# Scaling gathered rows by their decay: twelve ScalarE operations a group against three VectorE operations, from pass 12 on

## The chip, the core and the metric

The kernel runs on one core of a Trainium2 chip. Five engines work side by side, each through its own queue in order: PE (TensorE, matmul and transposition), ACT (ScalarE), DVE (VectorE), POOL (GpSimd, which here issues the gathers) and SP (SyncE, which issues the other transfers). They wait for one another through semaphores. The metric is device time in microseconds (us) of one launch.

## What is computed

One layer of attention over a graph with N = 12,500 nodes, D = 128 features and M = 200,000 edges that are sorted by target node. After a layernorm and a relu (the table `h`), each edge gets a score, decayed by the edge's own weight; per target node the 16 best edges are kept, a softmax is taken over them, and the source rows are summed with these weights:

```python
h = jnp.maximum(_layernorm(x, axis=-1), 0.0)
# in the layer, with node_feats = h:
Qv = node_feats @ W_Q.T
Ku = node_feats @ W_K.T
score = jnp.einsum('md,md->m', Qv[dst], Ku[src]) * (1.0 / np.sqrt(d))
score = score * jnp.exp(-DECAY_LAMBDA * edge_dt)
...
keep = rank < TOPK                      # the 16 best of each target node
w = jnp.where(keep, jnp.exp(score_m - seg_max[dst_s]), 0.0)
alpha = w / jnp.where(denom[dst_s] > 0, denom[dst_s], 1.0)
msgs = node_feats[src_s] @ W_msg.T
agg = jax.ops.segment_sum(alpha[:, None] * msgs, dst_s, num_segments=n)
x = x + jax.nn.relu(node_feats @ W_self.T + agg)
```

The decay multiplies a score, so it may as well multiply the edge's source row of `h` ahead of the product. That multiplication, row by row, is what the change moves.

## The kernel before

Edges are cut into chunks of 128 (one edge per partition) and groups of `GC = 12` chunks: 1,563 chunks, 131 groups. For group g the kernel does this:

- **Gather** (`gather`, line 194, POOL): one indirect DMA per chunk fetches 128 rows of `h_tab` by the edges' indices, which lie in the SBUF table `idx_all`, into `hs`, a tile of 128 x 12 x 128 floats. There are `HB = 10` such tiles. `gather_next(g + 10)` follows the sums of group g, and its first gather waits for the tile to be free.
- **Scale** (`scaled`, line 623, ACT): `hd = hs * dec`, one operation per chunk; the factor is one column of `dec_all`, a number for each partition. `hd` has two tiles.
- **Turn** (`edges_by_turns`, lines 217 and 655): PE transposes four chunks at a time from `hd` into a bank `t` of PSUM, and a copy brings them to `hdT`: the first four chunks by DVE, the others by ACT. Line 659 copies a strip that two groups share.
- **Score and search** (`scores`, `searched`): matmuls into the bank `s`, then DVE finds the 16 best (lines 692 to 703), ACT takes the exponentials (line 707), DVE forms the weights `wt` (713) and the reciprocal of their sum (718, 719).
- **Weights and sums** (`weights_turned`, `weights_out`, `sums`, `means`, `sums_out`): PE transposes `wt`, ACT copies it to `wT` (728), PE multiplies it with the rows in `hs`, ACT scales (753), PE transposes, ACT stores columns to `sum` (768). Blocks of 512 nodes are finished by products and the output on DVE (line 787).

The order on each queue is written out by hand. Passes run from i = -2 to `END = 119`; pass i scores and searches group i, turns group i + 1 and scales group i + 2. The last ten groups have a sequence of their own, in which the first chunks of a group are scaled by ACT and its last four by DVE (line 620). In a pass, `scale(n)` is called with 2, 3, 4, 4 and 12: it takes up to so many of the twelve chunks that are left, so two and three come ahead of the search, and the rest between and after. `T[g]["scaled", j]` keeps the instruction that scaled chunk j: PE's transpositions and the gather that reuses the tile wait for it.

Of the kernel before, what the change touches and what calls it, by code (L numbers as in the profile page):

```python
# [10 lines left out]
F32 = mybir.dt.float32  # L11
# [5 lines left out]
OP = mybir.AluOpType  # L17
# [6 lines left out]
P = 128  # L24
# [9 lines left out]
GC = 12  # L34
# [21 lines left out]
QB = 4  # L56
# [19 lines left out]
def bc(ap, n):  # L76

    return ap.unsqueeze(2).to_broadcast([ap.shape[0], ap.shape[1], n])
# [8 lines left out]
def gnn_layer(  # L87
# [27 lines left out]
    nc = tc.nc  # L115
    N, D = x.shape
# [60 lines left out]
    dec_all = const.tile([P, CW], F32, name="dec_all")  # L177
# [8 lines left out]
    own = [min(GC, CH - GC * g) for g in range(G)]  # L186

    T = [{} for _ in range(G)]
# [16 lines left out]
    def gathers_begun(gs, table, after=None):  # L205

        for g in gs:
            d = gather(g, 0, 1, lambda j: idx_all[:, GC * g + j:GC * g + j + 1], table)
            if after is not None:
                tc.add_manual_dep(d.ins, after.ins.name, SYNC, reason="behind a step of x's norms")  # L210
            gather(g, 1, own[g], lambda j: idx_all[:, GC * g + j:GC * g + j + 1], table)
# [86 lines left out]
    with tc.tile_pool(name="edges", bufs=1) as ep, ExitStack() as stage:  # L298
# [183 lines left out]
        for k in range(DW // FP):  # L482
            c = HALO + FP * k
# [6 lines left out]
        c = HALO + QE  # L490
# [51 lines left out]
    with tc.tile_pool(name="win", bufs=2) as win:  # L542
# [3 lines left out]
        def behind(d, product):  # L546
            if product is not None:
                tc.add_manual_dep(d.ins, product.ins.name, SYNC, reason="behind the last of some products")
# [59 lines left out]
        def load_rels(g):  # L608
            if g % RG == 0:
                d = nc.sync.dma_start(rels[g // RG % 2][0:2 * NQ, :].rearrange("k (g c) -> k g c", g=RG),  # L610
                                  m_rows[g:g + RG, :].rearrange("g (k c) -> k g c", k=2 * NQ))
                if g >= 2 * RG:
                    behind(d, T[g - RG - 1]["scored"])

        def scaled(g, *js, by=None):
            for j in js:
                if j == 0:
                    T[g]["hd"] = win.tile([P, GC, D], F32, name="hd", bufs=2)
                if j < own[g] and by is not None:
                    T[g]["scaled", j] = by(T[g]["hd"][:, j, :], T[g]["hs"][:, j, :],  # L620
                                           dec_all[:, GC * g + j:GC * g + j + 1], None, op0=OP.mult)
                elif j < own[g]:
                    T[g]["scaled", j] = nc.scalar.activation(T[g]["hd"][:, j, :], T[g]["hs"][:, j, :], AF.Copy,  # L623
                                                             scale=dec_all[:, GC * g + j:GC * g + j + 1])
            if g == 1 and 11 in js:
                gathers_begun((RAW + 2,), h_tab, T[1]["scaled", 11])
# [15 lines left out]
        def edges_by_turns(g, c, m=4, by=None, over=False):  # L642

            n = min(m, own[g] - c)
            if n > 0:
                turned_begun(g)
                pt = bank("t", 2)
                for j in range(n):
                    turn(pt[:, j * P:(j + 1) * P], T[g]["hd"][:, c + j, :], ident)
                    if j == 0:  # L650
                        behind(pe["last"], T[g]["scaled", c + n - 1])
                if over:
                    T[g - 1]["over"] = nc.scalar.copy(T[g - 1]["hdT"][:, GC * P:], pt[:, 0:HALO])
                out = by or (nc.vector.tensor_copy if c == 0 else nc.scalar.copy)
                T[g]["turned"] = out(T[g]["hdT"][:, c * P:(c + n) * P], pt[:, 0:n * P])  # L655

        def edges_over(g):
            if g:
                T[g - 1]["over"] = nc.scalar.copy(T[g - 1]["hdT"][:, GC * P:], T[g]["hdT"][:, 0:HALO])  # L659
# [130 lines left out]
        def store(b):  # L790
            o = B[b]["stored"] = B[b]["o"]
            n = min(N, BN * (b + 1)) - BN * b
            full = n // P
            if full:
                nc.sync.dma_start(out[BN * b:BN * b + P * full, :].rearrange("(t p) d -> p t d", p=P), o[:, 0:full, :])
            if n > P * full:
                nc.sync.dma_start(out[BN * b + P * full:BN * b + n, :], o[0:n - P * full, full, :])

        def at(g, stage, *args):
            if 0 <= g < G:  # L800
                stage(g, *args)
# [4 lines left out]
        def blocks(stage, when, i):  # L806
            for b in range(NB):
                if when[b] == i:
                    stage(b)
# [11 lines left out]
        END = G - LATE - 1  # L821
        lags = ((0, (0, 0, 1, 1)),)
        done = {stage: [] for stage in ("scores", "search", "sums", "means", "out")}

        def due(stage, before, i, lag):
            n = len(done[stage])
            while n < len(done[before]) and done[before][n] <= i - lag:
                if stage in ("means", "out"):
                    yield n
                else:  # L830
                    done[stage].append(i)
                    yield n
                n = len(done[stage])

        def some_sums(i, before):
            for g in due("sums", "search", i, before):
                while len(done["means"]) < g - 1:
                    some_means(i, len(done["means"]))
                weights_out(g)
                sums(g)  # L840

        def some_means(i, g):
            while len(done["out"]) < g - 1:
                some_out(i, len(done["out"]))
            means(g)
            done["means"].append(i)

        def some_out(i, g):
            sums_out(g)
            done["out"].append(i)  # L850

        for i in range(-2, END + 1):
            ls, lq, la, lo = [l for k, l in lags if k <= max(i, 0)][-1]
            by_pe = i + 1 >= 0 and True
            if i + 2 >= RG:
                at(i + 2, load_rels)
            blocks(load_h, [None] + need_q[1:], i + 8)
            for b in range(NB):
                if "o" in B[b] and "stored" not in B[b]:
                    store(b)  # L860

            for g in due("out", "means", i, lo):
                some_out(i, g)
            for g in due("means", "sums", i, la):
                some_means(i, g)
            some_sums(i, max(lq, 1))
            blocks(h_out, [None] + need_q[1:], i + 4)
            blocks(q_out, [None] + need_q[1:], i + 2)
            at(i, placed)
            if by_pe:  # L870
                for c in (0, 4, 8):
                    edges_by_turns(i + 1, c)
                edges_over(i + 1)
            unscored = list(range(len(done["scores"]), i + by_pe))

            def some_scores():
                while unscored and unscored[0] - 2 < len(done["search"]):
                    scores(unscored.pop(0), *range(NQ))
                    done["scores"].append(i)

            some_scores()
            turns = list(range(16)) if i + 1 >= 0 and not by_pe else []
            rows = list(range(GC))

            def edges(n):
                if turns:
                    edges_turned(i + 1, *turns[0:n])
                    del turns[0:n]

            def scale(n):  # L890
                if i < END:
                    scaled(i + 2, *rows[0:n])
                    del rows[0:n]

            scale(2)
            if ls == 0:
                edges(4)
                scale(3)
            for g in due("search", "scores", i, ls):
                searched(g, lambda: edges(2))  # L900
                scale(4)
                weights_turned(g)
                some_scores()
            assert not unscored
            edges(6)
            scale(4)
            if lq == 0:
                some_sums(i, 0)
            edges(16)
            scale(GC)  # L910
            if i + 1 > 0 and not by_pe:
                edges_over(i + 1)
            blocks(h_turned, [None] + need_q[1:], i + 6)
            blocks(q_made, [None] + need_q[1:], i + 4)
            for b in range(NB):
                if "po" in B[b] and "o" not in B[b] and B[b]["made"] <= i - lo:
                    output(b)
                if "po" not in B[b] and full_at[b] < len(done["out"]):
                    load_x(b)
                    products(b)  # L920
                    B[b]["made"] = i

            if 0 <= i + 3 - 2 and i + 3 < RAW and i + 3 >= 2:
                raw_stats(i + 3)
                raw_normed(i + 3)
            if i > 0 and later:
                later.pop(0)()
# [17 lines left out]
        for g in range(END + 2, G):  # L945
            p, i, r = g - 1, g - 2, g - 2
# [47 lines left out]
        p, g = G - 2, G - 1  # L994
# [201 lines left out]
```

## Time and profile before

| | |
|---|---|
| median of three runs | 1994.49 us (1992.88 to 1995.18) |
| the profiled execution, its own time | 1998.06 us |
| its span, first to last instruction | 1996.3 us |
| busy: PE / PEld / DVE / ACT / POOL | 1094.2 / 678.4 / 670.0 / 1117.1 / 1482.5 us |
| DVE, share of the span, instructions | 34%, 1,998 |
| ACT, share of the span, instructions | 56%, 3,822 |
| gathers from `h_tab` (line 194), POOL | 1,491, mean 945 ns |
| scaling on ACT (line 623) | 1,527 operations, 486.4 us busy, mean 391 ns |
| scaling on DVE (line 620, last groups) | 36 operations, 10.1 us busy, mean 311 ns |
| DMA, mean rate over the span | 71 GB/s |

A busy share is an average over a start of about 100 us, a long run of like passes and an end of its own; what limits a stretch is read from that stretch. "issue" in a list of waits means that the engine waited for nothing that the profile shows. In the timeline a line gives start, length, engine, line of the kernel, operation, what it writes and reads, how many instructions were merged, and in brackets the idle time ahead of it with what ended it.

### The profile page before, as it was taken

To read this page: it belongs to the slowest core of one execution; us is meant where nothing else is said; L and a number is where in the kernel's file an instruction comes from. 1 tells how busy PE (TensorE), PEld (TensorE's weight loads), DVE (VectorE), ACT (ScalarE), POOL (GpSimd) and SP (SyncE) were. 2 spreads that over 40 slices of the span, in tenths; PEclk is the share of its full clock that TensorE was granted. 3 is DMA by queue.
4 is the path that set the end of the run, shared out by engine and by line. 5 is a ranking of instruction groups with operands and counts; after the bars stand their busy time and mean duration, and the time that the engine had idled before them with its cause. 6 is when DMAs were issued, how large, how long until landed. Compare 5 with 4: busy or idle time off the path is not lost. (4 is left out here: it accounts for less than half of the span.)

```text
span 1996.3 us, 25211 instructions
## 1 busy us (share of the span) xinstructions
PE 1094.2 (55%) x7612; PEld 678.4 (34%) x7613; DVE 670.0 (34%) x1998; ACT 1117.1 (56%) x3822; POOL 1482.5 (74%) x1574
## 2 busy tenths in 40 slices
PE   0044656565665656556555565555555555555655
PEld 0022334333343333334334333333333333333333
DVE  7433232333333233232333323232232232232443
ACT  5876555655555555565555555555555555554543
POOL 7777777777777777777777777777777777777773
PEclk9955566776677756776577756766666566666676
DMA  9622222222222222222222222222222222222221
GB/s 225 203 64 64 54 70 64 59 69 70 54 70 70 54 70 65 58 70 69 54 69 70 56 68 70 54 70 70 54 70 61 62 69 54 70 59 61 66 65 34
DMA packets 96812, 140.93 MB, mean 71 GB/s; under 512 B 28774, under 2 KB 68055, under 8 KB 96164
## 3 DMA queue, kind: packets, MB, share of 16 engines
q0 software_dynamic: 50016, 102.53, 20.3%
q1 hardware_dynamic: 46654, 36.73, 6.9%
q8 instruction: 61, 1.00, 0.2%
q14 instruction: 81, 0.66, 0.1%
HBM read 125.41 MB, written 13.75 MB: 70 GB/s over the span
## 5 line engine op out<-in xcount | busy, mean ns | idle before, releaser
L194 POOL DMA_INDIRECT hs<-h_tab,idx_all x1491 | 1409.5, 945 | 454.5 <-issue 418.5
L623 ACT ACTIVATE hd<-hs,dec_all 128x128 f32<-128x128 f32 x1527 | 486.4, 391 | 103.4 <-DMA hs<-h_tab,idx_all 103.0
L217 PE MATMUL t<-ident,wt 128*128 128x128 f32 x524 | 141.5, 425 | 454.6 <-DVE wt L713 452.7
L655 DVE COPY hdT<-t 128x512 f32<-128x512 f32 (+1 forms) x140 | 92.3, 662 | 794.5 <-PE t L217 770.0
L217 PE MATMUL t<-ident,hd 128*128 128x128 f32 x1563 | 312.0, 356 | 72.8 <-ACT hd L623 47.2
L214 PE MATMUL acc<-hs,wT 128*32 128x128 f32 (+1 forms) x3646 | 275.4, 419 | 126.5 <-ACT wT L728 126.5
L217 PEld LDWEIGHTS t<-ident,hd 128*128 128x128 f32 x1563 | 255.6, 189 | 130.4 <-ACT hd L623 55.5
L655 ACT COPY hdT<-t 128x512 f32<-128x512 f32 (+2 forms) x261 | 151.1, 582 | 253.4 <-PE t L217 252.3
L217 PEld LDWEIGHTS t<-ident,wt 128*128 128x128 f32 x524 | 93.6, 216 | 564.7 <-issue 560.5
L214 PEld LDWEIGHTS acc<-hs,wT 128*32 128x32 f32 (+1 forms) x3646 | 170.6, 164 | 224.7 <-ACT wT L728 174.8
L692 DVE MAX8 v<-s 128x8 f32<-128x448 f32 x131 | 82.9, 633 | 410.2 <-PE s L214 406.9
L707 ACT ACTIVATE s<-s,nm 128x448 f32<-128x448 f32 x131 | 79.5, 607 | 186.2 <-DVE rest L697 186.2
L214 PE MATMUL s<-hdT,qh 128*32 128x448 f32 x1042 | 149.3, 645 | 0.0
L753 ACT ACTIVATE mean<-acc,rden 128x128 f32<-128x128 f32 x131 | 48.2, 368 | 177.9 <-PE acc L214 177.9
L768 ACT COPY sum<-acc 128x32 f32 x673 | 106.4, 188 | 19.6 <-PE acc L217 9.3
L728 ACT COPY wT<-t 128x512 f32<-128x512 f32 x131 | 76.0, 580 | 63.6 <-PE t L217 63.6
L214 PE MATMUL s<-rels,apart 9*128 9x448 bf16 x131 | 52.9, 404 | 104.9 <-ACT hdT L659 102.8
L713 DVE SCALAR_TENSOR_TENSOR wt<-rest,s 128x448 f32<-128x448 f32 x131 | 81.3, 621 | 23.1 <-ACT s L707 10.1
L602 ACT COPY qh<-qw 128x32 f32 x521 | 75.1, 217 | 17.1 <-issue 17.0
L700 DVE MAX8 v<-rest 128x8 f32<-128x448 f32 x131 | 82.3, 628 | 4.4
L194 POOL DMA_INDIRECT hs<-in_x_dram,idx_all x66 | 62.6, 949 | 26.9 <-issue 17.1
L697 DVE MATCH_REPLACE8 rest<-v,s 128x448 f32<-128x448 f32 x131 | 80.6, 615 | 0.0
(143 smaller groups left out, 905.6 us busy)
## 6 DMA issues: line engine op xcount, KB each, us to landing
hs<-h_tab,idx_all POOLq DMA_INDIRECT x1491
xb<-in_x_dram SPq DMA_DIRECT2D x24, 256.0 KB
out_dram<-o SPq DMA_DIRECT2D x24, 256.0 KB
hb<-h_tab SPq DMA_DIRECT2D x23, 256.0 KB
xg<-in_x_dram SPq DMA_DIRECT2D x20, 280.0 KB
h_tab<-xg SPq DMA_DIRECT2D x2, 1400.0 KB
h_tab<-xg SPq DMA_DIRECT2D x1, 1120.0 KB
hs<-in_x_dram,idx_all POOLq DMA_INDIRECT x66
```

The lines of the kernel that those rows point to most:

```text
L194: d = nc.gpsimd.indirect_dma_start(out=T[g]["hs"][:, j, :], out_offset=None, in_=table[0:N, :], in_offset=bass.IndirectOffsetOnAxis(ap=ind ...
L214: pe["last"] = nc.tensor.matmul(*args, **how)
L217: pe["last"] = nc.tensor.transpose(*args)
L623: T[g]["scaled", j] = nc.scalar.activation(T[g]["hd"][:, j, :], T[g]["hs"][:, j, :], AF.Copy, scale=dec_all[:, GC * g + j:GC * g + j + 1])
L655: T[g]["turned"] = out(T[g]["hdT"][:, c * P:(c + n) * P], pt[:, 0:n * P])
L692: nc.vector.max(v16[:, 0:8], ps)
L697: nc.vector.match_replace(rest, T[g]["v16"][:, 0:8], T[g]["ps"][:, 0:HW], LOW)
L700: nc.vector.max(T[g]["v16"][:, 8:16], T[g]["rest"])
L707: d = nc.scalar.activation(ps, ps, AF.Exp, bias=T[g]["nm"])
L713: nc.vector.scalar_tensor_tensor(wt[g % 3][:, 0:HW], T[g]["rest"], LOW, T[g]["ps"][:, 0:HW], op0=OP.is_equal, op1=OP.mult, accum_out=den)
L728: nc.scalar.copy(of(wT[g % 2], "q k"), of(T[g]["pw"], "k q"))
L768: d = nc.scalar.copy(B[b]["sum"][:, at_window(u, BN * b - MA, MA + BN + MA)], acc[g % 2][:, 1, QN * h:QN * (h + 1)])
```

## The change

From pass 12 on, `scale` no longer calls `scaled` but a new function, which multiplies four chunks (128 x 512 elements) by their factors in one DVE operation with two tensor inputs: the rows, and `dec_all` read with each factor repeated 128 times. It acts only when `scale` is called with four or more, so the calls with 2 and 3 do nothing, the two calls with 4 take four chunks each, and the last takes the remaining four. Passes before 12, and the last ten groups, are as before.

```diff
+        def scaled_four(g, c):
+            n = min(QB, own[g] - c)
+            if c == 0:
+                T[g]["hd"] = win.tile([P, GC, D], F32, name="hd", bufs=2)
+            if n > 0:
+                done = nc.vector.tensor_tensor(T[g]["hd"][:, c:c + n, :], T[g]["hs"][:, c:c + n, :],
+                                               bc(dec_all[:, GC * g + c:GC * g + c + n], D), op=OP.mult)
+                for j in range(c, c + n):
+                    T[g]["scaled", j] = done
...
             def scale(n):
-                if i < END:
+                if i < END and i >= 12:
+                    while n >= 4 and rows:
+                        scaled_four(i + 2, rows[0])
+                        del rows[0:4]
+                        n -= 4
+                elif i < END:
                     scaled(i + 2, *rows[0:n])
                     del rows[0:n]
```

(`QB` is 4.) This concerns the 107 passes from 12 to 118, groups 14 to 120. In the changed file the lines below the new function are 11 higher: 655 is 666, 692 is 703, 707 is 718, 719 is 730, 728 is 739.

On ACT's queue one such pass read so before, from the copy of the turned edges to the first stores of the sums (`s` is the bank of scores, `wT` the turned weights):

```order
L655 COPY hdT<-t 128x512 x2
L659 COPY hdT<-hdT 128x64
L623 ACTIVATE hd<-hs,dec_all 128x128 x5
L707 ACTIVATE s<-s,nm 128x448
L623 ACTIVATE hd<-hs,dec_all 128x128 x7
L728 COPY wT_81<-t 128x4x4x32
```

and with the change:

```order
L666 COPY hdT<-t 128x512 x2
L670 COPY hdT<-hdT 128x64
L718 ACTIVATE s<-s,nm 128x448
L739 COPY wT_81<-t 128x4x4x32
L779 ISA
L779 COPY sum<-acc_82 128x32
```

The twelve operations are gone from ahead of and behind the exponentials, and nothing takes their place. On DVE's queue the end of one search and the start of the next stood together before:

```order
L703 MATCH_REPLACE rest<-v_5703,rest 128x448
L713 SCALAR_TENSOR_TENSOR wt_79,den<-rest,s 128x448
L718 TENSOR_SCALAR rden<-den 128x1
L719 RECIPROCAL rden<-rden 128x1
L655 COPY hdT<-t 128x512
L692 MAX v_5823<-s 128x8
```

and now have the three multiplications between them:

```order
L714 MATCH_REPLACE rest<-v_5131,rest 128x448
L724 SCALAR_TENSOR_TENSOR wt_79,den<-rest,s 128x448
L729 TENSOR_SCALAR rden<-den 128x1
L730 RECIPROCAL rden<-rden 128x1
L621 TENSOR_TENSOR hd<-hs,dec_all 128x512 x3
L666 COPY hdT<-t 128x512
L703 MAX v_5229<-s 128x8
```

All three stand behind the search of group i and ahead of the copy of the next turned edges; each waits for the landing of its four gathers. Where a block is finished, its output (line 787 before) comes behind them. Nothing moves on POOL, PE and SP; PE's transpositions of `hd`, and the gathers that waited for ACT's last scaling, wait for DVE instead.

## The prediction

> **What bounds the kernel now.** I read the busy times first, then the groups of instructions, then POOL's own line by stage, and only then the passes.
>
> The two rows from the groups give the gathers and the operations to be replaced; the two below them, from the answer on line 194, give the shortest, median and longest gather.
>
> ```profile
> L194 POOL DMA_INDIRECT hs<-h_tab,idx_all x1491 | 1409.5, 945 | 454.5 <-issue 418.5
> L623 ACT ACTIVATE hd<-hs,dec_all 128x128 f32<-128x128 f32 x1527 | 486.4, 391 | 103.4 <-DMA hs<-h_tab,idx_all 103.0
> ...
> L194 POOL DMA_INDIRECT hs<-h_tab,idx_all x1491: 940/945/995, 102.6 to 1965.4; - x187
> L194 POOL DMA_INDIRECT hs<-in_x_dram,idx_all x66: 939/946/1072, 13.0 to 101.4; - x66
> ```
>
> POOL's 74% looks like slack, but its idle time is nearly all "issue", 0.30 us behind each gather: POOL waits for nobody. By stretches of line 194 (POOL busy, instructions in brackets) the pace is rigid:
>
> ```profile
> 0.00:300.00 300.00, 218.04 (x230) 0.72 0.44 113
> 300.00:1200.00 900.00, 680.67 (x720) 0.69 0.25 64
> 1300.00:1800.00 500.00, 378.07 (x400) 0.64 0.25 64
> ```
>
> 900/720 = 500/400 = 1.25 us a gather, 15.0 us a group. The last gather starts at 1965.4, and the chain of waits goes from there to the end:
>
> ```profile
> 1964.11 2.50 DMA hs<-h_tab,idx_all
> 1966.61 0.02 issue
> 1966.63 0.40 ACT hd L623
> ...
> 1988.75 0.42 DVE o L787
> ```
>
> So the time is 1,563 gathers one after another and some 31 us behind the last one. The passes are faster than the gathers. Line 719, once a pass, by stretches, and line 623 by stretches:
>
> ```profile
> 300.00:1200.00 900.00, 10.66 (x65) 0.69 0.25 64
> 1300.00:1800.00 500.00, 5.57 (x34) 0.64 0.25 64
> ...
> 0.00:300.00 300.00, 51.18 (x167) 0.72 0.44 113
> 300.00:1200.00 900.00, 239.52 (x775) 0.69 0.25 64
> ```
>
> A pass takes 900/65 = 13.85 us while it runs free. At 300 us scaling is 230 - 167 = 63 chunks behind the gathers; by 1200 it has made up 775 - 720 = 55 of them. Then the passes are bound to the landings: ACT begins to wait for them, a wait that the stretch from 300 to 1200 does not have.
>
> ```profile
> ACT hd L623 <- DMA hs<-h_tab,idx_all: 51.9, 72, 2.4
> ```
>
> **The change, part by part.** *What it removes.* 107 passes x 12 = 1,284 of the 1,527 operations of line 623. This is one free pass:
>
> ```profile
> 1004.09 1.57 ACT L623 ACTIVATE hd<-hs,dec_all 128x128 f32<-128x128 f32 x5
> ...
> 1006.37 0.61 DVE L697 MATCH_REPLACE8 rest<-v,s 128x448 f32<-128x448 f32 x1
> 1006.43 0.94 POOL L194 DMA_INDIRECT hs<-h_tab,idx_all  x1 [0.30 <-issue]
> ...
> 1007.08 0.61 ACT L707 ACTIVATE s<-s,nm 128x448 f32<-128x448 f32 x1 [1.42 <-DVE rest L697]
> 1007.61 2.14 ACT L623 ACTIVATE hd<-hs,dec_all 128x128 f32<-128x128 f32 x7
> ...
> 1009.32 0.16 DVE L719 RECIPROCAL rden<-rden 128x1 f32<-128x1 f32 x1
> ...
> 1010.37 0.59 ACT L728 COPY wT<-t 128x512 f32<-128x512 f32 x1 [0.62 <-PE t L217]
> ...
> 1013.99 1.15 PEld L217 LDWEIGHTS t<-ident,hd 128*128 128x128 f32 x8
> ...
> 1014.98 0.69 DVE L655 COPY hdT<-t 128x512 f32<-128x512 f32 x1 [4.89 <-PE t L217]
> ```
>
> 1.57 + 2.14 = 3.7 us of ACT a pass, 397 us in all, and worth nothing: ACT waits for others right behind both runs (1.42 us for the search, 0.62 for PE), and a pass that ended earlier would only reach the landings earlier.
>
> *What it adds on DVE's time.* Three operations a pass, 321 in all, 128 x 512 with two inputs. The nearest row is one with 521 elements a partition, 0.68 us (line 497, below); so 2.04 us a pass. They start behind line 719, at 1009.5 in the pass shown, and end by 1011.6; PE wants `hd` at 1013.99 and DVE itself sits idle for 4.89 us until the copy at 1014.98. Cover of 2.4 us: cost nothing. If it failed, the pass could still grow by 15.0 - 13.85 = 1.15 us. Queued behind the third operation are the copy of line 655 and, where a block is finished, the output of line 787. In a bound pass they now stand behind the landing of chunk 11: 0.68 instead of 0.40 for the scaling, then a copy of 0.69 that used to run earlier, about 1 us later, inside the 1.15. Nothing from group 121 on changes, so the 31 us stay.
>
> *What it adds on POOL's time.* This is the term. In the stretches of line 194 no gather of the passes lasts over 995 ns, whatever DVE does: MATCH_REPLACE at 1006.37, with one tensor input, runs across the start of the gather at 1006.43, which keeps its 0.94. The start of the kernel has DVE operations with two long tensor inputs in SBUF, as the new ones have:
>
> ```profile
> 28.12 0.94 POOL L194 DMA_INDIRECT hs<-in_x_dram,idx_all  x1 [0.30 <-issue]
> 28.51 0.68 DVE L429 TENSOR_TENSOR line<-row,line 1x521 f32<-1x521 f32 x1
> 29.37 0.95 POOL L194 DMA_INDIRECT hs<-in_x_dram,idx_all  x1 [0.30 <-issue]
> ...
> 97.06 0.68 DVE L497 TENSOR_TENSOR line<-line 1x521 f32<-1x521 f32 x1
> 97.51 1.05 POOL L194 DMA_INDIRECT hs<-in_x_dram,idx_all  x1 [0.30 <-issue]
> 98.87 0.94 POOL L194 DMA_INDIRECT hs<-in_x_dram,idx_all  x1 [0.30 <-DMA rels<-m_rows]
> ```
>
> Line 429 lies between the starts of two gathers, and costs neither anything. Line 497 lies across a gather's start and ends at 97.74, 0.23 us into it: the gather takes 1.05 instead of 0.945, and the next starts 1.36 us behind it, not 1.25. So 0.11 us is lost and not regained, as if the gather needed something at about 0.12 us from its start and had to wait for the end of the operation. I take it to be the reading of its indices.
>
> The Trainium skill, "SBUF — State Buffer", section "Who interferes with whom", says that a VectorE instruction with two SBUF inputs contends with a GpSimd instruction that reads SBUF, and not with one that only writes, and that who comes second blocks until the first has ended. By that rule line 497 is no accident, and the sum below is what it makes of this kernel; without the rule the sum would be nought.
>
> Price of one operation: a one-element operation takes 154 ns and line 497 takes 0.68, so 0.53 us of it are the reading.
>
> ```profile
> L693 DVE TENSOR_SCALAR nm<-v 128x1 f32<-128x1 f32 x131 | 20.1, 154 | 4.5
> ```
>
> A gather's moment falls into these 0.53 of every 1.25 us with chance 0.42, and then waits 0.27 us on average: 0.11 us an operation. Ends: nothing (line 429), and 0.53, if every one catches a gather at its start.
>
> While passes are free, phases drift, and a pass costs 3 x 0.11 = 0.34 us. Gathers then take 15.34 a group, so the passes catch up by 1.49 a pass; 55 chunks x 1.25 = 69 us need 46 passes: 46 x 0.34 = 16 us. The other 61 passes are bound. There the second and third operation start as their landing comes, and a landing comes 2.50 us from its gather's start, two gathers on, just at the start of another. The DVE operations of line 620, released in that way, show what follows:
>
> ```profile
> 1887.83 0.95 POOL L194 DMA_INDIRECT hs<-h_tab,idx_all  x1 [0.30 <-issue]
> 1887.85 0.28 DVE L620 TENSOR_SCALAR hd<-hs,dec_all 128x128 f32<-128x128 f32 x1 [0.96 <-DMA hs<-h_tab,idx_all]
> 1889.08 0.94 POOL L194 DMA_INDIRECT hs<-h_tab,idx_all  x1 [0.30 <-issue]
> ```
>
> It starts 0.02 us into a gather, which keeps its 0.95, so it comes too late to be in its way. I take nothing for these two, and 0.11 for the first, whose phase I don't know: 61 x 0.11 = 7 us.
>
> Sum: 16 + 7 = 23 us. Every microsecond lost on POOL is one of the end, since all gathers stand in one row. 1998.06 + 23 = 2021 for an execution like the profiled one; the median of the runs is 3.6 below it, so 1994.5 + 23 = 2018.
>
> **The rivals.**
> - *Not slower.* One hit is one hit: the operation of line 497 works on one partition, and the delay at 97.51 could have another cause; line 429 cost nothing. On the same page the skill says that an earlier probe saw `tensor_tensor` not stall a DMA, and infers that descriptor generation needs the write side alone. Then nothing is lost on POOL, DVE's 2.04 us are covered, and the time is 1994.5. It decides from a gather that keeps 0.945 across a new operation's middle. Against it: of 1,491 gathers none exceeds 995, so 1.05 isn't scatter. 0.13.
> - *Bound passes fall into a bad phase.* If the first operation in each of the 61 always catches a gather for 0.3 us or more, that is 18 instead of 7: 2030 to 2040. If the two released by landings come ahead of the reading after all and hold it for 0.5 each, it is 61 us more, 2080. For it: the phase is nearly the same in every bound pass. Against the second: the row at 1887.85. 0.14 and 0.05.
> - *DVE's queue becomes the bound.* If the 2.04 us lay on the path of a pass, it would take 15.9 instead of 15.0, and 107 x 0.9 = 96 us more: 2090. It decides from a cover under 0.9 us; the rows show 2.4. 0.03.
> - *Faster.* Gathers are put down to ACT's scaling 52 times, 15.9 us: were that a wait which goes away, 1979. But 15.9/52 is the 0.30 of "issue". 0.03.
>
> ```profile
> POOL hs L194 <- issue: 437.3, 1435, 0.3
> POOL hs L194 <- ACT hd L623: 15.9, 52, 0.3
> ```
>
> **How the numbers follow.** The forecast has 0.62, with a range of its own of 2003 to 2030 (9 to 36 us: 0.03 to 0.11 us an operation over all 321, the upper end without any help of the landings). With half of the first rival and the milder half of the second, 1995 to 2046 holds 8 in 10. About 0.2%, 4 us, is what a measurement can tell from no change. Slower: 0.62 + 0.14 + 0.05 + 0.03 = 0.84; same 0.13; faster 0.03.
>
> **What would show it.** Right: line 194's median stays at 945 but its mean rises by some 15 ns and its longest reaches 1.4 us or so, about one gather in fifteen is over 0.96 (the 46 x 3 + 61 operations of unknown phase, 0.42 of them), each of these with an operation of line 621 across its start; some 704 gathers in 900 us of free passes instead of 720; ACT idle by 3.7 us a pass more; passes of 13.85 us until about 950, and bound from there. Wrong: gathers of 945 throughout (no contention), or passes over 15 us with POOL waiting for DVE (the queue).

## The result, and the profile after

The changed kernel takes 2013.02 us (median of four runs, 2009.0 to 2015.13), the kernel before 1994.56 beside it: ratio 1.0091, 95% interval 1.0076 to 1.0106. The forecast was 2018. The profiled execution took 2012.88, with a span of 2011.1 us, 14.8 more than before.

The page of the changed kernel, busy times and groups: ACT went from 1117 to 733 us, DVE from 670 to 877, and POOL, whose instructions are the same, from 1482.5 to 1497.7.

```profile
PE 1105.3 (55%) x7612; PEld 674.7 (34%) x7613; DVE 877.4 (44%) x2319; ACT 732.7 (36%) x2538; POOL 1497.7 (74%) x1574
...
L194 POOL DMA_INDIRECT hs<-h_tab,idx_all x1491 | 1424.0, 955 | 454.4 <-issue 438.9
L621 DVE TENSOR_TENSOR hd<-hs,dec_all 128x512 f32<-128x512 f32 x321 | 210.9, 693 | 234.6 <-DMA hs<-h_tab,idx_all 232.7
```

A gather's mean rose from 945 to 955 ns while its median fell by one, so a few became much longer. The answer on line 194 (shortest, median, longest) and its stretches:

```profile
L194 POOL DMA_INDIRECT hs<-h_tab,idx_all x1491: 940/944/1464, 103.3 to 1980.5; - x187
...
300.00:1200.00 900.00, 682.39 (x715) 0.70 0.25 64
1300.00:1800.00 500.00, 379.01 (x398) 0.62 0.25 63
```

The longest was 995 before. In 900 us 715 gathers start where 720 did. The timeline shows who holds them. The first piece is a free pass, the second one bound to the landings:

```profile
641.51 1.90 DVE L621 TENSOR_TENSOR hd<-hs,dec_all 128x512 f32<-128x512 f32 x3
642.19 1.43 POOL L194 DMA_INDIRECT hs<-h_tab,idx_all  x1 [0.30 <-issue]
643.92 0.94 POOL L194 DMA_INDIRECT hs<-h_tab,idx_all  x1 [0.30 <-issue]
...
1685.35 0.69 DVE L621 TENSOR_TENSOR hd<-hs,dec_all 128x512 f32<-128x512 f32 x1
1685.64 1.23 POOL L194 DMA_INDIRECT hs<-h_tab,idx_all  x1 [0.30 <-issue]
1687.06 0.69 DVE L621 TENSOR_TENSOR hd<-hs,dec_all 128x512 f32<-128x512 f32 x1 [1.01 <-DMA hs<-h_tab,idx_all]
1687.17 1.40 POOL L194 DMA_INDIRECT hs<-h_tab,idx_all  x1 [0.30 <-issue]
1688.87 0.94 POOL L194 DMA_INDIRECT hs<-h_tab,idx_all  x1 [0.30 <-issue]
```

At 1685.64 a gather starts 0.29 us behind an operation's start and takes 1.23, 0.285 too long: 1685.64 + 0.12 + 0.285 is 1686.04, the operation's end. That sum (start, 0.12 and what the gather took too long) is called here the moment at which it resumes; a gather over 0.96 us counts as lengthened. Counted over all rows, 74 gathers are lengthened, by 17.2 us in all, 0.23 on average and 0.52 at most. All but one (0.06 us, in the last groups) belong to the passes, and these 73 resume within 0.06 us of the end of an operation of line 621. A gather that starts between about 0.04 and 0.55 us behind an operation's start is held; one outside is not (one at 0.60 took 0.017 longer). What a gather does at 0.12 us no row shows; that it reads its indices there, which lie in SBUF, is argued and not shown. So it closes: 17.2 us of lengthening, less 2.5 us because all other gathers stood 1.248 instead of 1.250 us apart in this execution, plus 0.4 us that were lost before pass 12, is the 15.1 us by which the last gather came later (1980.5 against 1965.4); the end behind it took 30.6 us against 30.9.

### The profile page after: what moved, and what is told of

Read it like the earlier page. It is cut to its first block, busy times and chain, and to the rows that moved or that the text cites. A ratio compares the mean times of both kernels' runs of the same rounds, so it can differ in the third digit from the quotient of the medians.

```text
span 2011.1 us, 25104 instructions
## 1 busy us (share of the span) xinstructions
PE 1105.3 (55%) x7612; PEld 674.7 (34%) x7613; DVE 877.4 (44%) x2319; ACT 732.7 (36%) x2538; POOL 1497.7 (74%) x1574
## 5 line engine op out<-in xcount | busy, mean ns | idle before, releaser
L194 POOL DMA_INDIRECT hs<-h_tab,idx_all x1491 | 1424.0, 955 | 454.4 <-issue 438.9
L217 PE MATMUL t<-ident,hd 128*128 128x128 f32 x1563 | 305.5, 349 | 119.7 <-DVE hdT L666 69.6
L621 DVE TENSOR_TENSOR hd<-hs,dec_all 128x512 f32<-128x512 f32 x321 | 210.9, 693 | 234.6 <-DMA hs<-h_tab,idx_all 232.7
L217 PEld LDWEIGHTS t<-ident,hd 128*128 128x128 f32 x1563 | 249.4, 185 | 177.0 <-DVE hdT L666 100.8
L718 ACT ACTIVATE s<-s,nm 128x448 f32<-128x448 f32 x131 | 79.5, 607 | 357.6 <-DVE rest L708 357.6
L739 ACT COPY wT<-t 128x512 f32<-128x512 f32 x131 | 76.6, 585 | 309.6 <-PE t L217 309.6
L214 PE MATMUL s<-hdT,qh 128*32 128x448 f32 x1042 | 161.3, 694 | 0.0
L634 ACT ACTIVATE hd<-hs,dec_all 128x128 f32<-128x128 f32 x243 | 79.4, 393 | 42.0 <-DMA hs<-h_tab,idx_all 41.8
```

The costliest lines, as they stand in the source:

```text
L194: d = nc.gpsimd.indirect_dma_start(out=T[g]["hs"][:, j, :], out_offset=None, in_=table[0:N, :], in_offset=bass.IndirectOffsetOnAxis(ap=ind ...
L214: pe["last"] = nc.tensor.matmul(*args, **how)
L217: pe["last"] = nc.tensor.transpose(*args)
L621: done = nc.vector.tensor_tensor(T[g]["hd"][:, c:c + n, :], T[g]["hs"][:, c:c + n, :], bc(dec_all[:, GC * g + c:GC * g + c + n], D), op=OP ...
L718: d = nc.scalar.activation(ps, ps, AF.Exp, bias=T[g]["nm"])
L739: nc.scalar.copy(of(wT[g % 2], "q k"), of(T[g]["pw"], "k q"))
```

## The experiments

The times of the first eight of the twelve runs can't be read like those of the first profile, so this comes first: on the two chips of the first eight runs the kernel before itself took 2411 and 2408 us. In the traces of those runs a pass took 17.5 us, and the release behind the sums (line 753) came some 4 us after the matmuls' modelled end, put down to "remote" (0.1 us in the first profile); about once a pass a gather waited too, for up to 4.4 us, so time lost on POOL could hide. The waits of the second run with one-input additions, below:

```profile
ACT mean L753 <- remote: 576.4, 115, 6.6
POOL hs L194 <- remote: 335.8, 118, 4.4
```

What these eight do show is the length of each gather, which does not hang on that. The last four ran on a chip with the first profile's times.

**Three more operations with two SBUF inputs, and three with one.** Both leave the kernel before as it is, with ACT's scaling, and add work on DVE behind the search:

```diff
                 searched(g, lambda: edges(2))
+                if 12 <= i < END:
+                    idle = win.tile([P, GC, D], F32, name="idle", bufs=1)
+                    for c in (0, 4, 8):
+                        nc.vector.tensor_tensor(idle[:, c:c + QB, :], T[g]["hs"][:, c:c + QB, :],
+                                                bc(dec_all[:, GC * g + c:GC * g + c + QB], D), op=OP.mult)
```

```diff
+                        nc.vector.max(idle[:, c, 0:8], T[g]["hs"][:, c:c + QB, :].rearrange("p c d -> p (c d)"))
```

> The kernel before, with ACT's scaling left as it was, and in passes 12 to 118 three VectorE multiplications more (two SBUF inputs, 128x512, the same place on the queue) on rows that have long landed; their result is not used. Theory A (a gather whose reading of its indices falls into an operation with two SBUF inputs waits for that operation's end): slower by about what the change lost, 12 to 25 us, so 2007 to 2020, and each long gather ends its wait with one of these operations. Theory B (the loss comes from taking the scaling off ACT, or from DVE waiting for landings): 1994.5, gathers at 945 ns throughout.

> As the run with three added multiplications, but the three added VectorE operations are a search for the eight largest over the same 512 elements: as long, the same place, one SBUF input; their result is not used. Theory A: 1994.5 within 2 us, no gather of the passes over 1.0 us. Theory C (any more work on DVE in this place costs time, whatever its inputs): as slow as the run with the multiplications.

Measured: 2415.33 and 2414.94 us against 2410.72, both 1.0021 (1.0012 to 1.003). The times tell the two apart in no way; the gathers do: 105 lengthened by 32 us in all with two inputs, none of the passes with one. Both ran again on another chip:

> The same kernel as the first run with three added multiplications (two SBUF inputs, result not used), since on the chip of those runs the kernel before itself took 2411 us, with passes of 17.5 us for which the gathers waited, so that time lost on POOL could hide. Where the kernel before takes its 1995 us: theory A, 12 to 25 us more; theory B (the loss comes from taking the scaling off ACT, or from DVE's waits for landings), none. Where it takes 2411 again: 110 or so long gathers again, worth some 33 us on POOL, and little of it in the time.

> The same kernel as the first run with three added operations of one SBUF input. Where the kernel before takes 1995 us: theory A, no change within 2 us; theory C (any work on DVE in this place costs time), as slow as the run with multiplications. In either place no gather of the passes is over 1.0 us.

The base was 2408.28; 2412.63 and 2412.55, both 1.0017 (1.0008 to 1.0026). Again 104 gathers, 33 us, against none. Line 194 of the two, two inputs first:

```profile
L194 POOL DMA_INDIRECT hs<-h_tab,idx_all x1491: 938/945/1449, 114.0 to 2316.9; - x187
...
L194 POOL DMA_INDIRECT hs<-h_tab,idx_all x1491: 938/944/957, 113.4 to 2316.5; - x187
```

So of operations as long and in the same place, those with two SBUF inputs lengthen gathers and the search with one does not; work on DVE as such, ACT's relief and waits for landings are out. The search also writes less, 8 elements a partition where the multiplication writes 512. That the long output is not the cause shows in the trace of the kernel before. Line 703 reads one long tensor from SBUF and writes one to SBUF; line 713 reads one from SBUF (`rest`) and one from PSUM (`s`):

```profile
812.59 0.62 DVE L713 SCALAR_TENSOR_TENSOR wt<-rest,s 128x448 f32<-128x448 f32 x1
812.66 0.94 POOL L194 DMA_INDIRECT hs<-h_tab,idx_all  x1 [0.30 <-issue]
...
1200.21 0.61 DVE L703 MATCH_REPLACE8 rest<-v,rest 128x448 f32<-128x448 f32 x1
1200.27 0.94 POOL L194 DMA_INDIRECT hs<-h_tab,idx_all  x1 [0.30 <-issue]
```

An operation of line 703 lies across the moment at 0.12 us of 42 gathers, one of line 713 of 34, and none of these gathers takes over 0.95 us. Another form with one SBUF input does hold gathers; that comes with the run of twelve such operations. Where gathers have slack, 33 us of lengthening cost nothing that can be seen. The 4 us that both kinds of addition cost there were not traced.

**One operation over twelve chunks.**

```diff
-            n = min(QB, own[g] - c)
+            n = min(GC, own[g] - c)
...
-                    while n >= 4 and rows:
-                        scaled_four(i + 2, rows[0])
-                        del rows[0:4]
-                        n -= 4
+                    if n == GC:
+                        scaled_four(i + 2, 0)
+                        del rows[0:GC]
```

> The changed kernel with one operation over all twelve chunks (128x1536, some 1.75 us) in place of three. Theory A: every operation is longer than a gather's period, so each catches one, for about 1.0 us in free passes and 0.4 to 0.5 in passes bound to landings, 60 to 70 us in all: 2050 to 2065, longest gather about 2.5 us. Theory D (a fixed price for each operation with two inputs, 18.5/321 = 0.058 us): 107 operations, 6 us, so 2000. Theory E (a price for each element read): as the change, 2013.

Measured: 2426.36 against 2410.72 us, 1.0049 (1.003 to 1.0068). In the profiled execution, the slowest of six (2414 to 2445), 103 gathers are lengthened, 1.11 us on average, 114 us in all:

```profile
L194 POOL DMA_INDIRECT hs<-h_tab,idx_all x1491: 942/947/2530, 115.4 to 2349.7; - x187
```

The longest is as theory A said: 2.53 us, 0.945 and nearly all of the 1.75 that the operation lasts. The price goes with the length of the hold, not with the number of operations (theory D) nor with the elements (theory E): the three added operations read as many, and held gathers for 32 us on this chip. Theory A's total was too low: it counted 0.4 to 0.5 us for passes that are bound to landings, while here 86 of the holds are over 1 us. Why they are so long in so many passes was not traced.

**Twelve operations of one chunk.**

```diff
-                done = nc.vector.tensor_tensor(T[g]["hd"][:, c:c + n, :], T[g]["hs"][:, c:c + n, :],
-                                               bc(dec_all[:, GC * g + c:GC * g + c + n], D), op=OP.mult)
...
+                    T[g]["scaled", j] = nc.vector.tensor_tensor(
+                        T[g]["hd"][:, j:j + 1, :], T[g]["hs"][:, j:j + 1, :],
+                        bc(dec_all[:, GC * g + j:GC * g + j + 1], D), op=OP.mult)
```

> The changed kernel with twelve operations of one chunk (128x128, two SBUF inputs, about 0.28 us each, 0.20 apart) in place of three of four. Theory A: a gather is caught about once a pass but waits 0.06 us on average, 0.11 at most: 6 us in all, 2000, longest gather about 1.06 us. Theory D (a fixed price for each operation): 1284 x 0.058 = 74 us, 2069. Theory E (a price for each element): 2013.

Measured: 2416.43 against 2410.72 us, 1.002 (1.0011 to 1.003). 124 gathers are lengthened, by some 25 us, most of them by 0.10 to 0.17 us, but 15 by 0.37 to 1.36. Theory A's 6 us and 1.06 us are refuted. The longest:

```profile
1587.82 2.10 DVE L622 TENSOR_TENSOR hd<-hs,dec_all 128x128 f32<-128x128 f32 x10
1588.43 2.31 POOL L194 DMA_INDIRECT hs<-h_tab,idx_all  x1 [0.30 <-issue]
1591.04 0.94 POOL L194 DMA_INDIRECT hs<-h_tab,idx_all  x1 [0.30 <-issue]
```

It resumes at 1588.43 + 0.12 + 1.36 = 1589.91, the end of the run of ten. The operations last 0.28 us each and start 0.20 apart, so they overlap in the trace. So a gather does not always get its turn when the operation that holds it ends: a run of short ones can hold it as one long one does. The three of the change, which overlap too, let it in at each end (its longest wait is 0.52). What decides it was not found.

**Twelve operations with one tensor input,** the form of line 620, in place of the four-chunk operation:

```diff
+                    T[g]["scaled", j] = nc.vector.tensor_scalar(
+                        T[g]["hd"][:, j, :], T[g]["hs"][:, j, :],
+                        dec_all[:, GC * g + j:GC * g + j + 1], None, op0=OP.mult)
```

> The changed kernel with twelve operations a pass of the form of line 620 (128x128, one tensor input, the factor as one column) in place of three with two tensor inputs. Theory A, by the rows of line 620 (36 operations, one gather longer by 0.05 us): 1284 of them lengthen some 36 gathers by 0.05, 2 us in all, so 1995 to 1998 where the kernel before takes 1995, and nothing over 1.05; the operations themselves wait for POOL instead, up to 0.51 us each. Rival F (an operation on DVE with SBUF input and output at this rate blocks the gathers as the two-input one does): 5 to 20 us more.

Measured: 2411.02 against 2408.28 us, 1.0012 (1.0003 to 1.0021). 85 gathers of the passes lengthened, by 7.5 us in all and 0.13 at most, and operations took longer as well, up to 0.478 us:

```profile
L622 DVE TENSOR_SCALAR hd<-hs,dec_all x1284: 266/278/478, 406.3 to 2267.6; 128x128 f32<-128x128 f32 x184
```

Theory A's 2 us is too low. Rival F is right about the block, though its price did not come: 84 of the 85 resume within 0.02 us of the end of one of these operations. The holds are short because the operations are. A longer one of the same kind holds longer; this is the start of the changed kernel, and ten of the fourteen traces have the like on line 439:

```profile
71.10 1.09 DVE L439 TENSOR_SCALAR m_r<-m_r 66x3584 bf16<-66x3584 bf16 x1
71.49 1.52 POOL L194 DMA_INDIRECT hs<-in_x_dram,idx_all  x1 [0.30 <-issue]
```

71.49 + 0.12 + 0.58 is 72.19, the operation's end. So one SBUF input is no safeguard by itself: `MAX8` and `MATCH_REPLACE8` let gathers pass, `TENSOR_SCALAR` from SBUF to SBUF holds them. Of the operations, 233 took over 0.31 us, and 146 of these end some 0.05 us behind a gather's end, as if they had waited for it. The lengthening of gathers is a quarter of what three two-input operations cause on the same chip (33 us). How this version would stand where gathers are the bound was not run.

**One of the three operations alone,** all other calls of `scale` going to ACT:

```diff
-                if i < END and i >= 12:
-                    while n >= 4 and rows:
-                        scaled_four(i + 2, rows[0])
-                        del rows[0:4]
-                        n -= 4
+                if i < END and i >= 12 and n == 4 and len(rows) == 7:
+                    scaled_four(i + 2, rows[0])
+                    del rows[0:4]
```

> The changed kernel with one of the three multiplications alone (chunks 5 to 8, behind the search); the other eight chunks of a group are scaled by ACT as before. Theory A with sharing (three operations in a row, 0.60 apart, catch at most one gather a pass, because a gather that waited comes too late for the third): 0.42 hits a pass of 0.25 us, 11 us in all, two thirds of the change's 17. Theory G (each operation costs the same, by itself): a third, 6 us. About 45 long gathers by the first, 25 by the second.

Measured: 2405.88 against 2408.28, 0.9996 (0.9987 to 1.0005), 54 long gathers, 13 us, against 104 and 33 for three. By count a half, by time two fifths, between the theories; passes of 17.5 us meet the gathers in other phases than those of the change. It was run again below.

**The same with gathers as the bound.** These leave out all but the first 8 sum matmuls of a group, which is to shorten the passes wherever they run. In `sums`:

```diff
+            parts = parts[:8]
             for i, (h, k) in enumerate(parts):
```

> The kernel before with only the first 8 of the up to 28 sum matmuls of a group, so that passes are short again on chips where the release behind the sums comes some 4 us later than in the first profile; the output leaves those sums out. It is the base of the three runs beside it. All theories: passes under 15.0 us, gathers 1.25 us apart and never waiting for a buffer, 1990 to 2010 in place of 2410.

> The changed kernel with the same sums left out as in the base. Theory A (two SBUF inputs hold back a gather's reading, and time lost on POOL is lost at the end once POOL is the bound): 12 to 30 us over the base, 60 to 105 long gathers, and the base's time plus the sum of their lengthening within 4 us. Theory B (the loss came from the order or from ACT's and DVE's waits): the lengthening of gathers and the loss of time do not agree.

> One multiplication of four chunks a pass, the other eight chunks on ACT, the same sums left out. Theory A with sharing (three in a row catch at most one gather a pass): 11 us over the base, two thirds of the loss of the change. Theory G (each operation costs the same by itself): 5 to 8 us, a third.

> The base with three added VectorE operations a pass, as long as the multiplications, at the same place, of one SBUF input; their result is not used, and the same sums are left out. Theory A: the base's time within 2 us, no gather of the passes over 1.0 us. Theory C (any work on DVE there costs time): 10 to 30 us over the base.

On this chip the kernel before took 1994.34 us, and the base 1993.77 (0.9998, 0.9989 to 1.0007): leaving out sums brings nothing, since passes are not the bound. The others, as ratios to the kernel before and as differences of medians to the base:

| | us | ratio, 95% | over the base | gathers lengthened | by, us |
|---|---|---|---|---|---|
| change | 2015.31 | 1.0117 (1.0099 to 1.0135) | 21.5 | 86 | 19.4 |
| one operation of the three | 2009.73 | 1.0083 (1.0069 to 1.0097) | 16.0 | 55 | 15.1 |
| three of one SBUF input added | 1993.42 | 1.0005 (0.9986 to 1.0024) | -0.3 | 1 | 0.02 |

The base itself has 4 gathers over 0.96 us, by 0.15 us in all. One of the control's eleven executions took 2012.73 us, the others 1990.4 to 1997.7; that one has no trace. Line 194 of the base, the change, the single operation and the one-input control:

```profile
L194 POOL DMA_INDIRECT hs<-h_tab,idx_all x1491: 940/944/1009, 103.6 to 1963.7; - x187
...
L194 POOL DMA_INDIRECT hs<-h_tab,idx_all x1491: 940/944/1417, 102.7 to 1982.2; - x187
...
L194 POOL DMA_INDIRECT hs<-h_tab,idx_all x1491: 940/944/1459, 100.0 to 1975.2; - x187
...
L194 POOL DMA_INDIRECT hs<-h_tab,idx_all x1491: 940/944/961, 103.0 to 1963.1; - x187
```

A pass of the control, with its three operations of one input across the starts of two gathers:

```profile
639.33 1.88 DVE L905 MAX8 idle<-hs 128x8 f32<-128x512 f32 x3
639.85 0.94 POOL L194 DMA_INDIRECT hs<-h_tab,idx_all  x1 [0.30 <-issue]
641.10 0.94 POOL L194 DMA_INDIRECT hs<-h_tab,idx_all  x1 [0.30 <-ACT sum L769]
```

Theory A holds: as many operations, as long, in the same place, cost nothing as searches with one SBUF input and 21.5 us as multiplications with two, and in the change's profiled execution the last gather came 18.5 us later than the base's for 19.4 us of lengthening. Theories B and C are out. A single operation costs three quarters of what three do (by the intervals, between half and all of it), so the three share their gathers, and theory G (a third) is out too. Theory A's own figure for the single one, 11 us, was too low as well: 16.0.

No experiment pointed to a version faster than the kernel before: its gathers already follow one another at 1.25 us without a break, and 1,563 x 1.25 = 1954 us of its time are theirs.

## Why the prediction was right, point by point

- **What bounds the kernel.** Right: removing 384 us of ACT's work brought nothing, and the loss on POOL came out at the end one for one. ACT now waits where it worked: 357.6 us for the search, 309.6 for PE's turned weights, where it had been 186.2 and 63.6.

```profile
ACT s L718 <- DVE rest L708: 357.6, 120, 3.8
ACT wT L739 <- PE t L217: 309.6, 126, 5.4
```

- **DVE's 2.04 us a pass are covered.** Right: from 300 to 1100 us there are 58 passes, 13.8 us each, against 13.85 before, and POOL waits for nothing. An operation takes 693 ns, as the row of line 497 said.
- **Gathers wait for operations with two SBUF inputs.** Right for the operations of the change, and shown by the pair with one and two inputs. The one held gather at 97.51 had all of it: the moment at 0.12 us, the end of the operation as the release, and no recovery. The Trainium skill, "SBUF — State Buffer", "Who interferes with whom", says so of a GpSimd instruction that reads SBUF: these runs agree (1 long gather, by 0.02 us, with one-input searches against 86 in the change, both where gathers are the bound). Its remark that `tensor_tensor` was seen not to stall a DMA does not carry over to a gather, which was held by up to 0.52 us here and by 1.59 us in the run of one operation. The number of inputs is not the whole rule: the longest gather of the second row of line 194 that the prediction shows, 1072 ns, started at 68.08 and resumed at 68.33, at the end (68.31) of a `TENSOR_SCALAR` of line 435 with one SBUF input. The prediction passed it over, and as line 435 does not run in the passes this changed nothing in its sum.
- **The size: 23 us forecast, 17.2 in the trace, 18.5 in the medians.** The term that was mis-sized is "a pass costs 3 x 0.11 = 0.34 us" in the free passes, 16 us: the trace has 8.5 there, in 60 passes up to 1140 us, so 0.14 a pass. One operation alone was not overrated: 55 hits in 107 passes of 0.275 us make 0.14 a pass, more than 0.11. But the three stand 0.60 us apart, within a period and a half of the gathers: one that is held resumes at an operation's end and is followed by the next 1.25 us later, too late for the third. At 641.51 above, the second operation holds the gather of 642.19, and the next starts at 643.92, when the run has ended at 643.41. Of the 68 passes with a long gather 5 have two. The third operation accounts for 3 of the 73. Sharing is not all of the shortfall: two operations that each hold a gather for 0.51 of 1.25 us, by 0.26 on average, would make an estimated 0.21 a pass, and the free passes of the run with 86 long gathers made 0.19 (9.1 us in 48 passes). The rest, down to 0.14, is the phases that this execution met, and was not explained.
- **Bound passes: 7 us forecast, 8.7 measured.** The first operation cost 5.4 of these, as a random phase would. The two that are released by a landing were to cost nothing, and cost 3.3: the row at 1687.06 shows why. The gather of 1685.64 had been held, so the next came late, the landing came ahead of it, and the operation it released started 0.11 us before the gather instead of behind its reading. The third operation, which waited for a landing in 50 of 107 passes, held three gathers in all, so that the landing's phase mostly spares them is borne out.
- **When the passes become bound.** Forecast about 950 us; measured between 1100, when the third operation begins to wait for its landing, and 1140, since POOL lost less than half as much in a free pass as I had put down. It moves both terms a little, in opposite ways.
- **About one gather in fifteen over 0.96.** 73 of the 1,284 gathers of these passes, one in 17.6. That the count came so near is partly luck: of the 84 forecast, 19 were to come from the third operation in free passes, where there was 1, and none from the second in bound passes, where there were 10.
- **The rivals.** "Not slower" rested on there being a single hit and on line 429, which cost nothing; the 73 hits and the control refute it. Of "bound passes fall into a bad phase" there is a trace in the 3.3 us. DVE's queue did not become the bound. "Faster" did not come: the 15.9 us that POOL's waits put down to ACT's scaling went to 1.2, and "issue" rose from 437.3 to 459.2.

## What to carry to other kernels

Where POOL's gathers are the bound, a VectorE operation with two SBUF inputs is priced on POOL's queue, not on its own: what counts is the chance that a gather's moment (0.12 us from its start) falls into the operation, and the length of the operation or of an unbroken run of short ones. Neighbouring operations share the gathers they catch, so here one cost three quarters of what three did. A form with one tensor input is not free of the price by that alone: `TENSOR_SCALAR` held gathers to its end, and twelve short ones a pass lengthened gathers by a quarter of what three long two-input ones did. Leaving the scaling on a ScalarE that has time costs nothing; relief of an engine that waits anyway buys nothing. Look for the gathers over 0.96 us, and at what ends when they go on, before you move work to VectorE.

## What the runs showed of the hardware that I had not expected

- A run of short two-input operations (0.28 us each, starting 0.20 apart) held a gather through the rest of one and six more, 1.36 us; operations of 0.69 us in the change let it in after each.
- A `TENSOR_SCALAR` with one SBUF input holds a gather to its end too: by up to 0.13 us where it lasts 0.28 (85 gathers, 7.5 us), by 0.58 where it lasts 1.09 (line 439). Such operations took up to 0.478 instead of 0.278 us beside gathers. `MAX8` and `MATCH_REPLACE8` with one SBUF input, and an operation with one input in SBUF and one in PSUM (line 713), hold none.
- In the runs on the two chips of the first eight the release behind the sums came about 4 us later than the matmuls' modelled end, and the kernel before took 2408 to 2411 us there in place of 1994. What does that was not found. Where passes take 17.5 us, gathers are not the bound, and up to 33 us of lengthening on POOL did not show in the time.
